# A graph layer on one Trainium2 core: node quarters chosen for each edge tile, seven sum slots a block for nine, and attention keys made in two steps a group

## The chip, the cores and the metric

One NeuronCore of a Trainium2 chip runs the program. Its engines work side by side and meet only through semaphores: TensorE (PE; its weight loads are shown as PEld), VectorE (DVE), ScalarE (ACT), GpSimd (POOL) and SyncE (SP). DMA transfers are issued from SP, ACT and POOL. The metric is the device time of one execution, in microseconds; the number given for a kernel is the median of its runs.

## The reference

Four layers follow one another over a table of 6,250 nodes of 256 values. Only the first one, and what prepares the second, is touched here:

```python
def _L0_gnn_ref(x, edge_index, edge_attr, u, batch, W1, b1, W2, b2):
    row, col = (edge_index[0], edge_index[1])
    h = jnp.concatenate([x[row], edge_attr], axis=1)
    h = jax.nn.relu(h @ W1 + b1)
    agg = jax.ops.segment_sum(h, col, num_segments=N_NODES)
    cnt = jax.ops.segment_sum(jnp.ones((h.shape[0],), h.dtype), col, num_segments=N_NODES)
    agg = agg / jnp.maximum(cnt, 1.0)[:, None]
    out = jnp.concatenate([x, agg], axis=1)
    return jax.nn.relu(out @ W2 + b2)
...
x = x + _L0_gnn_ref(_layernorm(x, axis=-1), edge_index, edge_attr_256, L0_gnn_u, batch0, L0_gnn_W1, L0_gnn_b1, L0_gnn_W2, L0_gnn_b2)
```

There are 106,250 edges, sorted by their destination `col`. For each edge the row of its source node is fetched, multiplied by one half of `W1`, added to the edge's attributes times the other half, passed through relu, and summed into the destination node. The second layer is a graph attention over 131,072 other edges with experts behind it; the third is a graph layer again over the first edges; the fourth is a mixture of experts. All is computed in float32.

## The kernel before

**Blocks, tiles, groups.** The nodes are cut into T = 49 blocks of P = 128. Since the edges are sorted, the edges of a block lie in one window: 18 tiles (CW) of 128 edges, beginning where the block's edges begin. A tile's edges are compared with the block's 128 node numbers (`equal`, L1211), which gives a matrix `eq` of 0 and 1, edges by nodes. The sum over edges is then a matmul: `eq` as the stationary operand, the edges' rows `h` (256 values and a 1 for the count) as the moving one, added up in one PSUM tile `pe` (`add_up`, L1522).

**Quarters.** Sorted edges also mean that the first tiles of a window hit only the first nodes of the block. So the 18 tiles are divided into six sets of three (NR, NT), and `QUARTERS` (L904) says which quarters of the block (32 nodes each) a set can hit. For each tile and quarter there is one matmul of 32 stationary columns, 33 in a block. The last block takes all 128 columns in one matmul of a tile. `load_windows` (L1183) counts how many edges lie inside their set's quarters; if the total isn't every edge, a slow general program runs behind this one.

**Groups.** Six tiles make a group (G1): set g and set g + 3. A block has NG = 3 groups, the layer 147. One turn of the main loop (L1632) has one number q and touches several groups at once: it joins group q-1, multiplies the attributes of group q, sums group q-2, starts the gathers of group q+2, turns the attributes of group q+1, and compares the edges of group q.

- `load_sources` (L1491): six indirect DMAs from POOL, each of 128 rows of 1 KB from `y_dram` into one of four buffers `h0` to `h3` (`ring`). A buffer is free when `add_up` of the group four before has read it.
- `load_attr` (L1401): the edge attributes, eight DMAs from SP and ACT into `ea`, three buffers.
- `turn` (L1497): DVE transposes `ea` into `et`. `hidden` (L1505): PE multiplies it with `w1b` into `ph` (two buffers of PSUM), in three parts of a turn (L1636, L1647, L1651).
- `join` (L1515): DVE adds `ph` to the gathered rows, ACT applies relu, in place.
- `add_up` (L1522): PE sums. In the old order of the loops, tile by tile from behind, the matmuls of the two sets alternate.
- `end_of` (L1547): after a block's third group, the mean, the second matmul and the first steps of the attention, spread over the following turns with `yield`.

**Work on the side.** `work`, `sort` and `slow` are lists of generators; `steps` (L1622) asks each for one step. `slow` finds and loads the windows of the next seven blocks. `sort` (L1614) prepares the attention: `make_keys` (L1259) packs source and destination of each attention edge into one number, in 8 x 6 = 48 steps, each a few DVE instructions on 128x128; `sort_steps` (L1295) sorts each partition's 1,024 numbers, in 100 steps of one or two DVE instructions; and `sorted_edges` (L1318) takes the result apart: nine DVE instructions on 128 x 640 to 848, five PE transposes, each with a copy by ACT into `lt` and a DMA to `low_dram`, and 160 short memsets with four comparisons. One step a turn: 148 steps and the tail for 149 turns.

**Order.** `Ordered.pin` (L35) ties each engine's instructions to the order in which the program was written, turn by turn. So an instruction that waits holds up all that stand behind it on its engine. In a turn PE has: part 0 of `hidden`, the sort's transposes if there are any, the sums, part 2, steps of `end_of`, part 4. DVE has: the join, a sort step, the turn of the attributes, steps of `end_of`, the comparisons, a window step. After the loop the layer's pools are given back and the attention starts, with the experts' matmuls of the second layer (L1715, L1731) between.

Of the kernel before, what the change touches and what calls it, by code (L numbers as in the profile page):

```python
# [8 lines left out]
F32 = mybir.dt.float32  # L9
# [7 lines left out]
P = 128  # L17
# [851 lines left out]
def kernel(ctx: ExitStack, tc: tile.TileContext, a: dict, out: bass.AP):  # L869
# [24 lines left out]
    CW = 18  # L894
# [7 lines left out]
    NR = CW // NT  # L902
    Q = P // 4
    QUARTERS = ((0, 1), (0, 2), (1, 3), (1, 4), (2, 4), (3, 4))  # L904
    H, X = a["L0_ffn_att_src"].shape
    HX = H * X
    GW = HX + 2 * H
# [36 lines left out]
    with ExitStack() as fast:  # L944
# [182 lines left out]
        def gather(dst, table, idx):  # L1127
            GP.indirect_dma_start(  # L1128
                out=dst, out_offset=None, in_=table[0:NP, :],
                in_offset=IndirectOffsetOnAxis(ap=idx, axis=0),  # L1130
            )

        def load_windows(b, pool):

            sl = slice(b * TB, (b + 1) * TB)
            n = TB * CW

            def flat3(v):
                return v.rearrange("p w a t -> p w (a t)")

            raw = {k: wix.tile([P, P], I32, name=f"raw_{k}") for k in ("src", "dst")}
            for w in range(b * TB, (b + 1) * TB):
                at, r = (w - b * TB) * CW, start_of(w)
# [38 lines left out]

            n = TB - (b == NB - 1)  # L1183
            for k, (lo, hi) in enumerate(QUARTERS):
                for limit, op in ((lo * Q - 0.5, OP.is_gt), (hi * Q - 0.5, OP.is_lt)):
                    if 0 < limit < P - 1:
                        V.scalar_tensor_tensor(
                            inside[:, :n, k, :], d[:, :n, k, :], limit, inside[:, :n, k, :],
                            op0=op, op1=OP.mult,
                        )  # L1190
# [20 lines left out]
        def equal(pool, w, q):  # L1211


            total = NT * Q * sum(hi - lo for lo, hi in (quarters(w, q), quarters(w, q + NG)))
            if w < T - 1:
                eq = pool.tile([P, EQ], F32, name="eq", bufs=3)
            else:
                eq = pool.tile([P, total], F32, name="eq4", bufs=1)
            found, at = {}, 0
            for k in (q, q + NG):  # L1220
                lo, hi = quarters(w, k)
                n = (hi - lo) * Q
                found[k] = eq[:, at : at + NT * n].rearrange("p (t n) -> p t n", n=n)
                at += NT * n
                V.tensor_tensor(
                    found[k], lane[:, None, lo * Q : hi * Q].to_broadcast([P, NT, n]),
                    dst1[:, w, k, :].unsqueeze(2).to_broadcast([P, NT, n]), op=OP.is_equal,
                )
            return found
# [88 lines left out]
        def sorted_edges(pst, wk):  # L1318
# [12 lines left out]
            for c in range(KA // P):  # L1331
                pt = pst.tile([P, 4, P], F32, name="pt")
                TE.transpose(pt[:, 0, :], some[:, c * P : (c + 1) * P], ident)
                lt = wk.tile([P, P], BF16, name="lt")
                SC.activation(lt, pt[:, 0, :], AF.Copy)
                SC.dma_start(low_dram[c * P : (c + 1) * P, :], lt)
            V.tensor_reduce(good2[:, 1:2], good3[:, :, 0], axis=AX.X, op=OP.add)
# [17 lines left out]
        with ExitStack() as layer:  # L1355
# [40 lines left out]
                return both  # L1396

            V.memset(gtab[:, :, HX : HX + H], 1.0)
            groups1 = [(w, g) for w in range(T) for g in range(NG)]

            def load_attr(q):  # L1401

# [66 lines left out]
            with (  # L1469
# [12 lines left out]
                last_of = [  # L1482
                    max(k % NG for k, (lo, hi) in enumerate(QUARTERS) if lo <= b < hi)
                    for b in range(4)
                ]
                NQ1 = len(groups1)

                def rows_of(q):
                    return ring[q % len(ring)]

                def load_sources(q):  # L1491

                    w, g = groups1[q]
                    for j, (k, t) in enumerate(chunk(g)):
                        gather(rows_of(q)[:, j, 0:D], y_dram, src1[:, w, k, t : t + 1])

                def turn(q):  # L1497

# [22 lines left out]

                def add_up(q):  # L1522

                    w, g = groups1[q]
                    if g == 0:
                        sums[w] = pse.tile([P, WS], F32, name="pe")
                    h, eq = rows_of(q), equals.pop(q)

                    for j in reversed(range(NT)):
                        for i, k in ((1, g + NG), (0, g)):  # L1530
                            lo, hi = quarters(w, k)
                            if hi - lo == 4:
                                TE.matmul(
                                    sums[w], eq[k][:, j, :], h[:, i * NT + j, 0:WS],
                                    start=g == 0 and j == NT - 1 and i == 1,
                                    stop=g == NG - 1 and j == 0 and i == 0,
                                )
                                continue
                            for b in range(lo, hi):
                                at = slice((b - lo) * Q, (b - lo + 1) * Q)  # L1540
                                TE.matmul(  # L1541
                                    sums[w][b * Q : (b + 1) * Q, :], eq[k][:, j, at],
                                    h[:, i * NT + j, 0:WS], start=g == 0 and j == NT - 1,
                                    stop=g == last_of[b] and j == 0,
                                )

                def end_of(w):  # L1547

# [64 lines left out]

                def sorting():  # L1614

                    yield from make_keys(wk)
                    yield from sort_steps()
                    sorted_edges(psm, wk)

                work, sort, slow = [], [sorting()], [windows()]  # L1620

                def steps(*more):  # L1622
                    for some in (*more, work):
# [2 lines left out]
                                some.remove(n)  # L1626

                for q in range(3):
                    load_sources(q)
                turn(0)  # L1630
                ordered = Ordered(tc)
                for q in range(NQ1 + 2):  # L1632
                    if 0 < q <= NQ1:
                        join(q - 1)
                    if q < NQ1:
                        hidden(q, 0)  # L1636
                    steps(sort)
                    if q >= 2:
                        add_up(q - 2)
                        if (q - 2) % NG == NG - 1:  # L1640
                            work.append(end_of((q - 2) // NG))
                    if 3 <= q + 2 < NQ1:
                        load_sources(q + 2)
                    if q + 1 < NQ1:
                        turn(q + 1)
                    if q < NQ1:
                        hidden(q, 2)  # L1647
                    steps()
                    if q < NQ1:
                        equals[q] = equal(wk, *groups1[q])  # L1650
                        hidden(q, 4)  # L1651
# [1019 lines left out]
```

## Time and profile before

| What | us |
|---|---|
| median of 3 runs (lowest, highest) | 3426.5 (3418.49, 3428.24) |
| the profiled execution, its own time | 3420.78 |
| its span, first to last instruction | 3418.8 |
| PE busy over the span | 3161.6 (92%) |
| DVE busy | 2156.1 (63%) |
| ACT busy | 1121.4 (33%) |
| POOL busy | 2245.7 (66%) |

The first layer's stream runs from about 104 us, when the first attributes are multiplied, to about 1277 us, when the last sum is done. The busy digits over 40 slices show it as the first 15 slices: PE at 8 and 9 tenths, DMA at 9, about 200 GB/s. In the last 1,000 us of the program the granted clock of PE is lower (5 to 7 tenths in the slices), which belongs to later layers.

How the rows are to be read: a row of the costliest groups has the line, the engine, the operation, the tile written and the tiles read, the shape and how often; then the busy time, the mean duration of one in ns, and the idle time of that engine just before such instructions with what ended most of it. "issue" means that nothing which the profile shows was waited for. A matmul of float32 has two records; records overlap, so the step from one to the next, not the duration of one, is what a matmul costs. Most matmuls stand under the line of a helper (L1115, L1109), gathers under L1128, and are told apart by their tiles.

### The profile page before, as it was taken

The numbers are of one execution on the slowest core, as the hardware profiler recorded it, in microseconds if no ns is written. First come the engines' busy times: TensorE is split into PE (matmuls) and PEld (weight loads), VectorE is DVE, ScalarE is ACT, GpSimd is POOL, SyncE is SP. The second block draws the span as 40 slices with busy tenths as digits, with TensorE's granted clock in tenths as the row PEclk, the third lists the DMA queues.
The fourth block names the chain that finished last, engine by engine and source line by source line (L and its number), as shares of the span: only waits on it lengthen the run. The fifth ranks groups of instructions, "written<-read, shape, count | busy, mean of one in ns | idle before, by whom it ended". The sixth has DMA issues, their size and how long they took to land.

```text
span 3418.8 us, 57189 instructions
## 1 busy us (share of the span) xinstructions
PE 3161.6 (92%) x18509; PEld 2529.4 (74%) x18509; DVE 2156.1 (63%) x5685; ACT 1121.4 (33%) x2010; POOL 2245.7 (66%) x2364
## 2 busy tenths in 40 slices
PE   7899999999999989999999999995678888988998
PEld 5677777777777767888888888883556665666776
DVE  5677787777666767877575758775334444545464
ACT  4122222222222224445545455661012112111134
POOL 0677777777777736766565556625777777777773
PEclk8999999999999999999999999996577777778698
DMA  6999999999999953334343434443112222222221
GB/s 190 199 210 204 199 199 206 200 199 203 206 208 207 207 119 102 98 87 132 85 118 99 132 85 132 113 100 88 53 54 59 60 59 60 59 59 65 60 63 39
DMA packets 698912, 428.56 MB, mean 125 GB/s; under 512 B 531272, under 2 KB 640315, under 8 KB 698604
## 3 DMA queue, kind: packets, MB, share of 16 engines
q0 software_dynamic: 89408, 178.08, 22.9%
q1 hardware_dynamic: 365948, 187.21, 21.0%
q10 hardware_dynamic: 243248, 59.52, 9.6%
q8 instruction: 150, 2.46, 0.3%
q14 instruction: 158, 1.29, 0.1%
HBM read 382.05 MB, written 42.49 MB: 124 GB/s over the span
## 4 chain that ended last, share of the span: by engine, by line
PE 65%; POOL 13%; DMA 9%; issue 6%; DVE 4%; ACT 2%; SPq 0%; ACTq 0%; POOLq 0%; DVEq 0%
PE ph L1115 33%; POOL hg L1128 12%; PE py L1115 11%; DMA hg<-hp_dram,src 6%; PE pe L1541 6%; PE po L1884 5%; PE pt L1115 4%; PE pe L2526 2%; DMA rb<-low_dram 2%; PE pa L1821 1%; PE pm L1115 1%; PE pt L1109 1%; POOL h L1128 1%; DMA h<-y_dram,src 1%; DVE x_all L2065 1%
## 5 line engine op out<-in xcount | busy, mean ns | idle before, releaser
L1128 POOL DMA_INDIRECT h<-y_dram,src x882 | 844.0, 957 | 395.0 <-issue 263.8
L1128 POOL DMA_INDIRECT hg<-hp_dram,src x831 | 784.5, 944 | 268.9 <-issue 221.2
L1128 POOL DMA_INDIRECT sg<-gat_dram,src x640 | 612.3, 957 | 353.0 <-issue 161.3
L1115 PE MATMUL ph<-w1b,et 128*128 128x256 f32 x3528 | 825.6, 386 | 10.4 <-DVE et L1500 9.9
L1115 PEld LDWEIGHTS ph<-w1b,et 128*128 128x128 f32 x3528 | 657.5, 191 | 153.6 <-issue 70.2
L2526 PEld LDWEIGHTS pe<-eq,hg 128*128 128x128 f32 x2036 | 392.8, 256 | 306.1 <-issue 134.4
L2526 PE MATMUL pe<-eq,hg 128*128 128x96 f32 (+15 forms) x2036 | 451.1, 351 | 159.0 <-DMA hg<-hp_dram,src 135.9
L1519 ACT ACTIVATE h<-h 128x1536 f32<-128x1536 f32 x147 | 218.2, 1485 | 586.5 <-DMA h<-y_dram,src 203.8
L2503 DVE TENSOR_SCALAR eq<-px,dst,ew 128x96 f32<-128x96 f32 x831 | 262.0, 367 | 232.5 <-PE pe L2526 142.4
L1518 DVE TENSOR_TENSOR h<-ph,h 128x1536 f32<-128x1536 f32 x147 | 258.3, 1757 | 228.2 <-PE ph L1115 208.4
L1115 PE MATMUL py<-w,hh 128*128 128x256 f32 x1568 | 385.6, 386 | 5.4 <-ACT hh L1720 4.9
L1115 PE MATMUL ph<-b_all,w 128*128 128x256 f32 (+1 forms) x1600 | 386.9, 381 | 2.9 <-issue 2.8
L1115 PEld LDWEIGHTS py<-w,hh 128*128 128x128 f32 x1568 | 290.6, 192 | 41.9 <-ACT hh L1720 6.9
L1115 PEld LDWEIGHTS ph<-b_all,w 128*128 128x128 f32 x1600 | 291.3, 191 | 36.2 <-issue 3.2
L1500 DVE STREAM_TRANSPOSE et<-ea 128x1536 f32<-128x1536 f32 x147 | 260.9, 1775 | 14.8 <-DMA ea<-in_edge_attr_dram 8.9
L1720 ACT ACTIVATE hh<-ph,b 128x256 f32<-128x256 f32 (+1 forms) x400 | 166.0, 466 | 289.0 <-PE ph L1115 276.2
L1884 PE MATMUL po<-pp,B 128*128 128x240 f32 (+10 forms) x1280 | 252.1, 337 | 1.9 <-DVE acc L1890 1.8
L1884 PEld LDWEIGHTS po<-pp,B 128*128 128x128 f32 x1280 | 215.5, 190 | 14.1 <-DVE acc L1890 2.6
L1541 PE MATMUL pe<-h,eq 128*32 128x257 f32 x3168 | 216.8, 384 | 0.0
L1863 DVE TENSOR_TENSOR pp<-px,A 128x960 f32<-128x960 f32 (+10 forms) x160 | 155.8, 974 | 3.9 <-PE po L1884 3.5
L1541 PEld LDWEIGHTS pe<-h,eq 128*32 128x32 f32 x3168 | 95.9, 109 | 83.9 <-issue 30.5
L1720 ACT ACT_TABLE_LOAD x98 | 125.7, 1283 | 49.7 <-PE ph L1115 47.1
(339 smaller groups left out, 3762.6 us busy)
## 6 DMA issues: line engine op xcount, KB each, us to landing
ea<-in_edge_attr_dram SPq DMA_DIRECT2D x588, 96.0 KB
ea<-in_edge_attr_dram ACTq DMA_DIRECT2D x588, 96.0 KB
y<-y SPq DMA_DIRECT2D x196, 128.0 KB
w<-in_L_ffn_W_dram SPq DMA_DIRECT2D x48, 512.0 KB
y<-ys SPq DMA_DIRECT2D x96, 256.0 KB
rb<-low_dram SPq DMA_DIRECT2D x80, 256.0 KB
h<-y_dram,src POOLq DMA_INDIRECT x882
hg<-hp_dram,src POOLq DMA_INDIRECT x831
```

Of the source, the lines that this page charges most:

```text
L1109: TE.transpose(pt[:, c, :], src[:, c * P : (c + 1) * P], ident)
L1115: TE.matmul(dst, lhs(c), rhs(c), start=c == 0, stop=c == n - 1)
L1128: GP.indirect_dma_start(out=dst, out_offset=None, in_=table[0:NP, :], in_offset=IndirectOffsetOnAxis(ap=idx, axis=0),)
L1500: V.transpose(et[q].rearrange("p c m k -> p m c k"), ahead.pop(q).rearrange("p i m (c k) -> p (i m) c k", c=2),)
L1518: V.tensor_add(h, ph.pop(q), h)
L1519: SC.activation(h, h, AF.Relu)
L1541: TE.matmul(sums[w][b * Q : (b + 1) * Q, :], eq[k][:, j, at], h[:, i * NT + j, 0:WS], start=g == 0 and j == NT - 1, stop=g == last_of[b] a ...
L1720: SC.activation(hidden[u][:, f, :n, :], ph[:, f - f0, :n, :], AF.Gelu, bias=b1[:, e, f : f + 1],)
L1863: V.tensor_tensor(pps[g, half][:, :, 0:n, :], pay[:, js, :].unsqueeze(2).to_broadcast([P, HG, n, HV]), near[g][:, js, 0:n].unsqueeze(3).to ...
L1884: TE.matmul(po.rearrange("p b v -> p (b v)"), B[:, j, :], pp[:, j, 0:n, :].rearrange("p b v -> p (b v)"), start=half == 0 and j == 0, stop ...
L2503: V.tensor_scalar(equals[k][:, j, :], lanes[:, 0:NW], dst_of[:, t : t + 1], ew[:, t : t + 1], op0=OP.is_equal, op1=OP.mult,)
L2526: TE.matmul(sums[b][:, lo - t0 * P : hi - t0 * P], hg[:, j, :], eq[:, j, lo - n0 : hi - n0], start=False, stop=after >= (t0 + n) * P,)
```

## The change

1. Each tile gets its own set of quarters (`reach`, from `RANGES`), 26 pairs of tile and quarter instead of 33. The test in `load_windows` goes over runs of tiles with the same limit.
2. The groups of a block are taken in the order 2, 0, 1 (`TURNS`). A plan made once (`planned`) hands out the pairs: 2, 2 and 3 slots (`SLOTS`) in the three turns, a slot having at most one matmul for each quarter. What doesn't fit, at most the third tile of either set (`LATE1`), is summed one or two turns later; so its rows and its part of `eq` are kept on.
3. `load_sources` is called twice a turn: for the tiles in `LATE1` of group q+1, then for the other four of group q+2.
4. `eq` has four buffers instead of three, the last block uses two of them in place of `eq4`, and `lt` has one buffer instead of two.
5. `make_keys` is a list of its own, `keys`, of which a turn takes two steps, one before the sums and one after part 2 of `hidden`. The sort starts when it is done.

```diff
-    groups1 = [(w, g) for w in range(T) for g in range(NG)]
+    TURNS, SLOTS = (2, 0, 1), (2, 2, 3)
+    RANGES = (((0, 1), 3), ((0, 2), 2), ((1, 2), 2), ((1, 3), 3), ((2, 3), 1), ((2, 4), 3), ((3, 4), 4))
+    reach = [r for r, n in RANGES for _ in range(n)]
+    groups1 = [(w, g) for w in range(T) for g in TURNS]
...
-            for k, (lo, hi) in enumerate(QUARTERS):
-                for limit, op in ((lo * Q - 0.5, OP.is_gt), (hi * Q - 0.5, OP.is_lt)):
-                    if 0 < limit < P - 1:
-                        V.scalar_tensor_tensor(
-                            inside[:, :n, k, :], d[:, :n, k, :], limit, inside[:, :n, k, :],
+            for limit in range(1, 4):
+                for op, some in (
+                    (OP.is_gt, [j for j in range(CW) if reach[j][0] == limit]),
+                    (OP.is_lt, [j for j in range(CW) if reach[j][1] == limit]),
+                ):
+                    part = slice(some[0], some[-1] + 1)
...
-                eq = pool.tile([P, EQ], F32, name="eq", bufs=3)
-            else:
-                eq = pool.tile([P, total], F32, name="eq4", bufs=1)
+                if eq is None or w == T - 1:
+                    eq, at = pool.tile([P, EQ], F32, name="eq", bufs=4), 0
...
-                lt = wk.tile([P, P], BF16, name="lt")
+                lt = wk.tile([P, P], BF16, name="lt", bufs=1)
...
+                def planned():
+                    left, plan, first, final = [[] for _ in range(4)], [], {}, {}
+                    for i, g in enumerate(TURNS):
+                        for j, (k, t) in enumerate(chunk(g)):
+                            for b in range(*reach[k * NT + t]):
+                                left[b].append((i, j, k, t))
+                        for n in range(SLOTS[i]):
+                            for b in range(4):
+                                if left[b]:
+                                    plan.append((i, b, *left[b].pop(0)))
...
+                LATE1 = (NT - 1, 2 * NT - 1)
+                EARLY1 = tuple(j for j in range(G1) if j not in LATE1)
...
-                    for j in reversed(range(NT)):
-                        for i, k in ((1, g + NG), (0, g)):
-                            lo, hi = quarters(w, k)
...
-                            for b in range(lo, hi):
-                                at = slice((b - lo) * Q, (b - lo + 1) * Q)
-                                TE.matmul(
-                                    sums[w][b * Q : (b + 1) * Q, :], eq[k][:, j, at],
-                                    h[:, i * NT + j, 0:WS], start=g == 0 and j == NT - 1,
+                    for i, b, own, j, k, t, start, stop in plan:
+                        if i == turn:
+                            of = q - turn + own
+                            lo = QUARTERS[k][0]
+                            TE.matmul(
+                                sums[w][b * Q : (b + 1) * Q, :],
+                                equals[of][k][:, t, (b - lo) * Q : (b - lo + 1) * Q],
+                                rows_of(of)[:, j, 0:WS], start=start, stop=stop,
...
                 def sorting():
-                    yield from make_keys(wk)
                     yield from sort_steps()
                     sorted_edges(psm, wk)
-                work, sort, slow = [], [sorting()], [windows()]
+                work, keys, sort, slow = [], [make_keys(wk)], [sorting()], [windows()]
...
-                    steps(sort)
+                    steps(keys or sort)
                     if q >= 2:
                         add_up(q - 2)
...
+                    if 3 <= q + 1 < NQ1:
+                        load_sources(q + 1, LATE1)
                     if 3 <= q + 2 < NQ1:
-                        load_sources(q + 2)
+                        load_sources(q + 2, EARLY1)
...
-                    steps()
+                    steps(keys)
```

More of the change, by code (lines that the diff above doesn't have):

```diff
@@ L1183, in load_windows @@
             n = TB - (b == NB - 1)
-            for k, (lo, hi) in enumerate(QUARTERS):
-                for limit, op in ((lo * Q - 0.5, OP.is_gt), (hi * Q - 0.5, OP.is_lt)):
-                    if 0 < limit < P - 1:
-                        V.scalar_tensor_tensor(
-                            inside[:, :n, k, :], d[:, :n, k, :], limit, inside[:, :n, k, :],
-                            op0=op, op1=OP.mult,
-                        )
+            tiled, at = (v.rearrange("p w a t -> p w (a t)") for v in (inside, d)), 0
+            tiled = list(tiled)
+            for limit in range(1, 4):
[4 more added lines that the diff above has]
+                    part = slice(some[0], some[-1] + 1)
+                    assert len(some) == some[-1] + 1 - some[0]
+                    V.scalar_tensor_tensor(
+                        tiled[0][:, :n, part], tiled[1][:, :n, part], limit * Q - 0.5,
+                        tiled[0][:, :n, part], op0=op, op1=OP.mult,
+                    )
             if n < TB:
@@ L1211, in equal @@
         def equal(pool, w, q):
-            total = NT * Q * sum(hi - lo for lo, hi in (quarters(w, q), quarters(w, q + NG)))
-            if w < T - 1:
-                eq = pool.tile([P, EQ], F32, name="eq", bufs=3)
-            else:
-                eq = pool.tile([P, total], F32, name="eq4", bufs=1)
-            found, at = {}, 0
+            eq, found, at = None, {}, 0
             for k in (q, q + NG):
@@ L1480 @@
                 equals, et, ph, sums = {}, {}, {}, {}
[L1482 to L1485, printed above, removed]
+                def planned():
[8 more added lines that the diff above has]
+                                    plan.append((i, b, *left[b].pop(0)))
+                        assert all(v[0] == i and v[1] in LATE1 for some in left for v in some)
+                    assert not any(left)
+                    for n, v in enumerate(plan):
+                        first.setdefault(v[1], n)
+                        final[v[1]] = n
+                    return [
+                        (*v, n == first[v[1]], n == final[v[1]]) for n, v in enumerate(plan)
+                    ]
+                LATE1 = (NT - 1, 2 * NT - 1)
+                EARLY1 = tuple(j for j in range(G1) if j not in LATE1)
+                plan = planned()
                 NQ1 = len(groups1)
@@ L1489, in rows_of, with load_sources @@
                     return ring[q % len(ring)]
-                def load_sources(q):
+                def load_sources(q, some):
                     w, g = groups1[q]
                     for j, (k, t) in enumerate(chunk(g)):
-                        gather(rows_of(q)[:, j, 0:D], y_dram, src1[:, w, k, t : t + 1])
+                        if j in some:
+                            gather(rows_of(q)[:, j, 0:D], y_dram, src1[:, w, k, t : t + 1])
                 def turn(q):
@@ L1522, in add_up @@
                 def add_up(q):
[L1524 to L1525 removed]
+                    w, turn = groups1[q][0], q % NG
+                    if turn == 0:
                         sums[w] = pse.tile([P, WS], F32, name="pe")
[L1527 to L1545 removed]
+                    if w == T - 1:
+                        for j, (k, t) in enumerate(chunk(TURNS[turn])):
+                            TE.matmul(
+                                sums[w], equals[q][k][:, t, :], rows_of(q)[:, j, 0:WS],
+                                start=turn == 0 and j == 0, stop=turn == NG - 1 and j == G1 - 1,
+                            )
+                        return
+                    for i, b, own, j, k, t, start, stop in plan:
+                        if i == turn:
+                            of = q - turn + own
+                            lo = QUARTERS[k][0]
+                            TE.matmul(
+                                sums[w][b * Q : (b + 1) * Q, :],
+                                equals[of][k][:, t, (b - lo) * Q : (b - lo + 1) * Q],
+                                rows_of(of)[:, j, 0:WS], start=start, stop=stop,
+                            )
                 def end_of(w):
@@ L1628 @@
                 for q in range(3):
-                    load_sources(q)
+                    load_sources(q, range(G1))
                 turn(0)
```

## The prediction, made before the changed kernel had run

> **What bounds the kernel now.** The change touches only the first layer, so I read that stage by itself: first the table of busy time by stretches, then the chain of waits inside it, then the instructions in order of time. In the table each engine has its busy us and, in brackets, its instructions; the last three columns are granted clock, DMA share and GB/s.
>
> ```profile
> 104.00:250.00 146.00, 138.81 (x912) 106.23 (x911) 112.36 (x221) 37.99 (x56) 110.65 (x117) 0.99 1.05 205
> 800.00:1240.00 440.00, 440.00 (x2945) 342.69 (x2939) 308.19 (x515) 126.09 (x211) 328.85 (x344) 1.00 0.96 203
> 1240.00:1300.00 60.00, 47.51 (x249) 38.54 (x247) 30.91 (x228) 19.14 (x43) 1.30 (x3) 0.91 0.24 67
> ```
>
> From 800 to 1240 us PE is never idle. POOL, the fifth engine, looks free with 328.85 of 440 us, but it isn't:
>
> ```profile
> L1128 POOL DMA_INDIRECT h<-y_dram,src x882 | 844.0, 957 | 395.0 <-issue 263.8
> L1541 PE MATMUL pe<-h,eq 128*32 128x257 f32 x3168 | 216.8, 384 | 0.0
> ```
>
> A gather takes 957 ns and 263.8 us / 882 = 0.30 us of issue before it: 1.256 us, so 18 gathers a block take 22.6 us. The order of time shows the gathers one behind the other, with one short wait:
>
> ```profile
> 1206.55 0.94 POOL L1128 DMA_INDIRECT h<-y_dram,src  x1 [0.30 <-issue]
> 1207.80 0.95 POOL L1128 DMA_INDIRECT h<-y_dram,src  x1 [0.30 <-issue]
> 1209.32 0.94 POOL L1128 DMA_INDIRECT h<-y_dram,src  x1 [0.58 <-issue]
> ```
>
> The third starts 1.52 us after the second, not 1.25: the sums of a block (until 1208.55 below) had to give it its buffer. PE's own period is in the chain:
>
> ```profile
> 1192.53 3.65 PE ph L1115 x16
> ...
> 1207.11 1.44 PE pe L1541 x24
> 1208.55 5.38 PE ph L1115 x24
> 1214.15 1.43 PE pe L1541 x18
> 1215.58 3.65 PE ph L1115 x16
> ```
>
> The same piece comes back after 1215.58 - 1192.53 = **23.05 us**, PE's block. POOL's 22.6 stands 0.45 us under it. So PE is the bound, and POOL is right behind. DMA is not third in line: in the packets an edge-attribute tile lands some 14 us before it is turned, although the share is 0.96.
>
> **Part 1: seven slots for nine.** Four 32-column matmuls, one for each quarter of the nodes, run side by side. The 24 records of a group (12 matmuls, two records each) take 1.44 us; 18 records (3 quarters) take 1.43. So a group costs three slots, however many quarters are in each. One record: (5.38 - 3.65) / 8 = 0.216 us from the ph rows, the same step as between the records of a slot in the trace; a slot is 2 x 0.216 = 0.432 us, and 1.44 - 3 x 0.432 = 0.14 us of entry stays. Before: 3 + 3 + 3 slots. After: 2 + 2 + 3, with 6 + 8 + 12 = 26 matmuls instead of 33. Removed: 2 x 0.432 x 48 blocks = **41.5 us of PE**; the last block is summed with whole matmuls as before. PE's block becomes 23.05 - 0.86 = 22.19 us, **under POOL's 22.6**. POOL makes the same 882 gathers, so POOL is late next.
>
> Neither the comparisons that make `eq` nor the window tests change in cost (six tests for seven, 176 ns each, seven times: 1 us of DVE, hidden below PE). The sets hold every edge of the inputs: I counted all 106,250 in them, so the general path is not entered.
>
> **Part 2: gathers in two parts, tiles kept for a group longer.** Tiles 2 and 5 of a group are now gathered one step later and stand in the order two of them, then four of the next. Same instructions, same queue. From the sum that frees the buffers to the join that needs the late tiles there are two steps instead of three, but they are first in the queue: 2 x 1.25 + 2.8 us of landing (mean over all gathers, from the packets; 5.3 us at the 99th percentile). PE needs the join's `ph` buffer 18.9 us after the release (two and a half steps of 7.4), and 6.4 us of DVE work stand before that in DVE's order (the join, sort steps, block end, turn), so they may land 12.5 us after it. With 5.3 that leaves about 7 us for POOL to be behind. I cost it at nothing; without that cover every landing tail costs its excess, about 2 us.
>
> The new cost is waits. In the program before, one gather of a group waits for PE; now five or six of six do: 668 waits on PE instead of 143. For POOL, the nearest row is the last layer's gathers (hg), of which every sixth waits for a DMA and PE: the trace has a semaphore instruction of 17 ns there, and the distance to the gather ahead stays 1.245 us, like the rest (1.249). So 0; upper end 0.1 us each, if POOL doesn't hide it (rival D). For PE, the Trainium skill speaks against this (TensorE: Matmul & The Clock Gate, "The cost: per-tile semaphore tail"): increments from matmuls serialize, 26.3 ns each. By it, 525 more increments cost 13.8 us of PE, 0.29 a block. The row: at the end of a ph group a matmul that increments is followed 0.215 us later, the usual step, so 0. I take the row; by the page PE's block would be 22.48, still under POOL's 22.6, so the sum would hardly differ.
>
> **Part 3: keys in two steps a group.** 48 key steps of 0.84 us DVE (152 instructions, 40.3 us in the trace) go into 24 groups instead of 48. DVE has 112.36 of 146 us there, 77%; 0.84 more in 7.6 us makes 88%: hidden behind PE and POOL, 0 to 2 us if DVE's order holds back a turn. But the sort behind them (100 steps) then ends at group 125 of 147 instead of in the last step, and with it the tail that sorts out the edges moves **from the end into the middle of the stream**. What it does at the end now:
>
> ```profile
> 1257.42 1.75 DVE L1518 TENSOR_TENSOR h<-ph,h 128x1536 f32<-128x1536 f32 x1
> ...
> 1262.57 0.49 DVE L1321 TENSOR_SCALAR src<-order 128x640 int32<-128x640 int32 x1
> ...
> 1267.42 0.60 DVE L1330 CAST low<-key 128x848 bf16<-128x848 f32 x1
> ```
> ```profile
> 1267.81 0.28 ACT L1335 ACTIVATE lt<-pt 128x128 bf16<-128x128 f32 x1 [4.44 <-PE pt L1333]
> ...
> 1269.68 0.28 ACT L1335 ACTIVATE lt<-pt 128x128 bf16<-128x128 f32 x1 [0.88 <-DMA low_dram<-lt]
> ...
> 1272.34 4.82 PE L1533 MATMUL pe<-h,eq 128*128 128x257 f32 x12
> ```
>
> The last join ends at 1259.2; the last sum could start 1.5 us later (ACT's relu) and starts at 1272.34: 11.6 us. Experts' matmuls fill part of it. PE idles 60 - 47.51 = 12.5 us in this stretch, of which the tail holds some 7, and its five transposes 1: **8 us go**, since PE is full again afterwards.
>
> In the middle it costs more. Queued behind it on PE: the sum of group 123, which frees POOL's buffers. Conversions 5.4 us on DVE, of which PE covers 2 with matmuls; then five transposes, each waiting for ACT's copy, which waits for the landing of the copy before, since `lt` now has one buffer: 1.5 us at the end, when DMA was quiet (1268.12 to 1269.6), and I take 2 to 3 beside full traffic. 4 + 5 x 0.6 + 4 x 2.5 = **17 us of PE**, ends 10 and 25. POOL goes on for its 7 us of lead, so 10 us reach the end of the stage.
>
> **The sum,** from join to join of the profiled execution (first 108.3, last 1257.4):
> - blocks 0 to 7: before 188.5 us; POOL 8 x 22.7 = 182: 6 gained.
> - blocks 8 to 27, where loading windows disturbs every seventh: before 477.9; PE 477.9 - 20 x 0.86 = 460.6, POOL 453, partly absorbing one another: 462, 16 gained.
> - the last 20.7 blocks: before 476.4 (23.05 each); POOL 20.7 x 22.65 = 469, and 10 of the tail: 3 lost.
> - the end: 8 gained.
>
> 6 + 16 - 3 + 8 = 27; 3420.8 - 27 = 3394. The profiled execution lies 5.7 under the median of the runs (3426.5); I add half of that: **3397 us**. The rest of the program is untouched.
>
> **Rivals.**
> - A, the forecast, 3384 to 3412: chance 0.55.
> - B, POOL doesn't bind: its 1.25 us contain waits that shrink, and its lead swallows the tail (5 us left): 41.5 + 8 - 5 = 45, so 3379. For it: the gathers' median step is 1.251, 22.5 a block. Against: 22.5 is still over 22.19. 0.17.
> - C, nothing to measure: the tail costs 25 us of PE, none absorbed, and keys and late tiles 4: 6 + 16 + 8 - (25 + 4 - 7) = 8 gained, 3416. For it: PE, ACT and DVE wait for one another there, with one buffer each. 0.16.
> - D, slower: POOL pays for the added waits. Some 12 gathers of a block at 0.1 us: 22.65 + 1.2 = 23.85, over 48.7 blocks 1161 us against 1149, and 10 - 8 for the tail: 14 lost, 3437. It decides from 0.076 us a wait. For it: where a gather really waits, 0.3 us go. Against: the hg row. 0.10.
> - E, 0.02: a set of quarters misses edges and the slow path runs; the count speaks against it.
>
> Under 0.3% (10 us) this kernel can't be told from no change. Faster: A, B and a little of C, 0.75; same 0.13; slower 0.12. The range 3375 to 3424 leaves out D and half of B.
>
> **What would show it.** The sums have 2,496 records in 128x32 form, in pieces of 12, 16 and 24. Right: gathers 1.25 to 1.27 us apart through the stage, PE idle some 0.4 us a block, blocks of 22.6; one hole of 10 to 25 us on PE around 1060 us; the last sum within 4 us of the last join. Wrong: blocks of 22.2 (B), gathers over 1.33 apart (D), blocks still 23.05 (the slots cost no less).

## The result and the profile after

The changed kernel takes **3401.09 us** (median of 5 runs, 3400.27 to 3405.05), the kernel before on the same chip 3422.54 (median of 5, 3418.49 to 3428.24; the 3426.5 given ahead is the median of three of them): ratio 0.9939, 95% interval 0.9924 to 0.9954, 21 us or 0.6% faster. The profiled execution's span fell from 3418.8 to 3401.3, by 17.5 us.

First the two groups of the costliest list that the change touches (busy us, mean ns of one, then the idle time just before them and what ended it).

```profile
L1131 POOL DMA_INDIRECT h<-y_dram,src x882 | 848.8, 962 | 393.6 <-issue 197.3 <-DMA ea<-in_edge_attr_dram 92.0 <-PE pe L1564 48.8
L1564 PE MATMUL pe<-h,eq 128*32 128x257 f32 x2496 | 178.4, 390 | 0.0
```

The sums fell from 3,168 records to 2,496. The gathers are as many and as long as before. 48.8 us of their idle time is now put down to waits for PE's sums. Part of this is no added cost, since 0.30 us stands before any gather; the rest are longer waits, like the one of 7.29 us shown further down. The same stretches as before the change:

```profile
104.00:250.00 146.00, 137.38 (x836) 105.37 (x836) 126.30 (x284) 38.43 (x57) 110.61 (x117) 0.98 1.01 207
800.00:1240.00 440.00, 423.52 (x2648) 329.70 (x2647) 305.67 (x647) 126.45 (x211) 326.20 (x338) 0.98 0.98 201
1240.00:1300.00 60.00, 56.91 (x338) 48.37 (x337) 31.91 (x92) 24.61 (x50) 20.50 (x22) 0.97 0.41 109
```

In the first, DVE's 112.36 has become 126.30 (the keys, twice as dense); in the second, PE, which was never idle, is idle for 16.5 us in all; in the third, PE has 56.91 instead of 47.51. The chain in an undisturbed stretch gives PE's block:

```profile
1134.79 3.65 PE ph L1118 x16
...
1141.89 1.00 PE pe L1564 x16
1142.90 5.38 PE ph L1118 x24
...
1148.49 1.44 PE pe L1564 x24
...
1156.97 3.65 PE ph L1118 x16
```

1156.97 - 1134.79 = **22.18 us** for 23.05. Two of the three pieces of sums now take 1.00 us instead of 1.43, the third 1.44. The gathers beside them, in order of time, come 1.25 us apart, also the one for which a wait for the sums is recorded (0.30 us, as where nothing is waited for):

```profile
1147.53 0.95 POOL L1131 DMA_INDIRECT h<-y_dram,src  x1 [0.30 <-issue]
...
1148.79 0.95 POOL L1131 DMA_INDIRECT h<-y_dram,src  x1 [0.31 <-PE pt L1112]
...
1150.04 0.95 POOL L1131 DMA_INDIRECT h<-y_dram,src  x1 [0.30 <-PE pe L1564]
```

So the slots cost what they were priced at, 0.86 us a block or 41.5 us in all, while the whole change gained 21. By the joins' starts in the trace (times between joins, so that each stretch can be compared; the last join began at 1257.42 and at 1251.84):

| Stretch | before | after | gained | predicted |
|---|---|---|---|---|
| up to the first join | 108.25 | 106.63 | 1.6 | 0 |
| blocks 0 to 7 | 188.48 | 188.93 | -0.5 | 6 |
| blocks 8 to 27 | 477.87 | 474.08 | 3.8 | 16 |
| block 28 to the last join | 482.8 | 482.2 | 0.6 | -3 |
| last join to the end | 2161.4 | 2149.4 | 12.0 | 8 |

The tail is where it was expected. In the instructions by time (in brackets the idle time before each, with what ended it):

```profile
1077.03 0.45 PE L1339 MATMUL pt<-ident,key 128*128 128x128 f32 x1 [5.77 <-DVE key L1335]
...
1080.40 0.28 ACT L1341 ACTIVATE lt<-pt 128x128 bf16<-128x128 f32 x1 [2.61 <-DMA low_dram<-lt]
...
1086.86 0.69 PE L1112 MATMUL pt<-ident,o 128*128 128x128 f32 x2 [1.36 <-ACT lt L1341]
...
1087.48 1.94 PE L1564 MATMUL pe<-h,eq 128*32 128x257 f32 x12
...
1089.28 1.40 POOL L1131 DMA_INDIRECT h<-y_dram,src  x1 [7.82 <-issue]
```

PE waits 5.8 us for the conversions, then for each transpose's copy, whose `lt` waits for the store ahead (2.61 us the longest). The sum behind them begins at 1087.48, and POOL, its lead used up, has stood for 7.8 us (the row puts this down to "issue"; that it waits for the sum is read from the order). This block takes 39.95 us, **17.8 more** than 22.18. At the end the reverse:

```profile
1251.84 1.76 DVE L1544 TENSOR_TENSOR h<-ph,h 128x1536 f32<-128x1536 f32 x1 [3.94 <-DMA h<-y_dram,src]
...
1256.93 2.77 PE L1555 MATMUL pe<-h,eq 128*128 128x257 f32 x12
...
1277.35 0.95 POOL L1131 DMA_INDIRECT sg<-gat_dram,src  x1 [4.27 <-DMA hp<-in_src_dram]
```

The last sum follows the last join's end by 3.3 us instead of 13, and the attention's first gather comes 25.5 us after the join's start instead of 41.8 (1299.20 in the trace of before).

### The profile page after: what moved, and what is told of

The parts are those of the page before. It is cut to its first block, busy times and chain, and to the rows that moved or that the text cites. A ratio compares the mean times of both kernels' runs of the same rounds, so it can differ in the third digit from the quotient of the medians.

```text
span 3401.3 us, 56400 instructions
## 1 busy us (share of the span) xinstructions
PE 3126.4 (92%) x17837; PEld 2510.2 (74%) x17837; DVE 2154.8 (63%) x5678; ACT 1121.5 (33%) x2010; POOL 2251.3 (66%) x2364
## 4 chain that ended last, share of the span: by engine, by line
PE 56%; DMA 15%; POOL 13%; issue 7%; DVE 5%; ACT 2%; SPq 1%; ACTq 0%; POOLq 0%; DVEq 0%
PE ph L1118 28%; POOL hg L1131 12%; PE py L1118 11%; DMA hg<-hp_dram,src 6%; PE po L1908 5%; DMA ea<-in_edge_attr_dram 4%; PE pe L1564 4%; PE pt L1118 3%; DMA h<-y_dram,src 3%; PE pe L2550 2%; DMA rb<-low_dram 2%; PE pa L1845 1%; DVE et L1526 1%; PE pt L1112 1%; PE pm L1118 1%
## 5 line engine op out<-in xcount | busy, mean ns | idle before, releaser
L1118 PEld LDWEIGHTS ph<-w1b,et 128*128 128x128 f32 x3528 | 658.6, 191 | 160.9 <-issue 75.0
L1564 PE MATMUL pe<-h,eq 128*32 128x257 f32 x2496 | 178.4, 390 | 0.0
L1118 PE MATMUL py<-ew,g 65*128 65x256 f32 x392 | 132.7, 469 | 1.0 <-DVE miss L2640 1.0
```

The lines of the kernel that those rows point to most:

```text
L1118: TE.matmul(dst, lhs(c), rhs(c), start=c == 0, stop=c == n - 1)
L1564: TE.matmul(sums[w][b * Q : (b + 1) * Q, :], equals[of][k][:, t, (b - lo) * Q : (b - lo + 1) * Q], rows_of(of)[:, j, 0:WS], start=start, s ...
```

## Where the gain of blocks 8 to 27 went

The table of stretches, cut at the joins of these 20 blocks, first of the kernel before, then of the changed one (busy PE, PEld, DVE, ACT, POOL; then clock, DMA share, GB/s):

```profile
296.73:774.60 477.87, 468.11 (x3093) 361.83 (x3094) 360.48 (x699) 131.12 (x221) 343.35 (x359) 0.99 0.99 201
```
```profile
295.56:769.65 474.09, 453.21 (x2813) 352.60 (x2814) 357.74 (x668) 130.62 (x221) 344.45 (x358) 0.98 1.04 202
```

PE does 14.9 us less and is idle 20.9 us instead of 9.8: most of what the slots gave came back as idle PE. Neither is it POOL at its limit: 344.45 us of gathers and 358 x 0.30 of issue are 451.9 of 474.1. The idle time stands in a few places, every 14 turns, where SP loads the windows of the next seven blocks with 14 small transfers (`raw_src`, `raw_dst`, L1149). There are four such batches in these blocks, and the waits of PE for ACT beside them, 3.53, 4.33, 1.77 and 6.80 us, are 16.4 of the 20.9 us; in the kernel before they are 2.04, 0.67 and 2.75 us at three of the batches, 5.5 together. The longest one of the changed kernel, in order of time:

```profile
728.05 5.28 ACTq L1416 DMA_DIRECT2D ea<-in_edge_attr_dram  x4
...
731.59 0.28 SPq L1149 DMA_DIRECT2D raw_dst<-in_dst_dram  x1
...
733.60 1.48 ACT L1545 ACTIVATE h<-h 128x1536 f32<-128x1536 f32 x1 [11.32 <-DMA raw_src<-in_src_dram]
...
735.41 2.08 PE L1118 MATMUL pt<-w,b_all 128*128 128x256 f32 x4 [6.80 <-ACT o L1113]
...
742.15 0.94 POOL L1131 DMA_INDIRECT h<-y_dram,src  x1 [7.29 <-PE pe L1564]
```

ACT's four issues of edge attributes take 5.28 us; two turns later, undisturbed, 1.89. Its relu, whose join was ready at 730.4, and its copy of `o` stand behind them, PE waits 6.80 us for the copy, POOL 7.29 us for the sum behind that. And PE then starts slowly:

```profile
735.40:741.20 5.80, 5.79 (x16) 4.51 (x16) 1.62 (x5) 1.60 (x2) 0.00 (x0) 0.62 1.25 207
741.20:760.00 18.80, 18.80 (x126) 14.56 (x125) 12.22 (x21) 5.00 (x10) 13.57 (x15) 1.00 0.82 184
```

The granted clock is 0.62 in the 5.8 us after the wait, 1.00 after that. The Trainium skill has a rule for this (TensorE: Matmul & The Clock Gate, "Why this matters for your kernels"): no idle gap of PE over some 3 us, or the clock falls back. The trace agrees for this gap, but the limit is not sharp here: in the changed kernel the clock was 1.00 in the 6.4 us after the wait of 3.53 us, and in the kernel before it was 0.68 in the 5.3 us after the one of 2.04:

```profile
405.38 1.40 PE L1115 MATMUL pt<-w,b_all 128*128 128x256 f32 x4 [2.04 <-ACT o L1110]
```
```profile
405.40:410.70 5.30, 5.30 (x16) 4.08 (x16) 2.20 (x8) 1.48 (x2) 1.92 (x3) 0.68 1.22 227
```

From here the theory to test, **T**: the slots' gain is given back by these loads (30.5 us over 20 x 22.18 in blocks 8 to 27, where the kernel before lost 16.9 over 20 x 23.05), by the tail's 17.8 us, and by POOL's limit of about 22.6 us a block once its lead is gone. Against it stand D (the added waits and late gathers cost time themselves), R (POOL sets the pace, so the tail's place doesn't matter) and W (the loads are not the cause).

## The experiments

**The loads spread** (loads_spread). A pair of loads a turn, instead of 14 in one turn:

```diff
                     SY.dma_start(v[at : at + CW, :], rows)
-            for _ in range(3):
-                yield
+                yield
+            yield
```

> The changed kernel with the 14 loads of a batch of windows (raw_src, raw_dst, issued by SP in one step, 1.5 us each) spread over seven steps, a pair each. Theory T: the long blocks (25 to 31 us, about every fifth up to block 27) come from SP standing in these loads, so that ACT's edge-attribute issues, and its relu and copies behind them, come late: they shrink to below 24 us each, blocks 8 to 27 take 450 to 460 us instead of 474: 3380 to 3390 us. Rival W (the long blocks come from the windows' arithmetic on DVE, or from the gathers that stand late in POOL's queue): 3397 to 3405 us.

Measured: 3383.53 us, ratio 0.9875 (0.9859 to 0.9892). Blocks 8 to 27:

```profile
287.41:743.48 456.07, 448.88 (x2817) 350.14 (x2816) 348.99 (x636) 131.16 (x220) 346.75 (x359) 1.00 1.03 209
```

18 us less than in the changed kernel, at a clock of 1.00, and now POOL is at its limit: 346.75 + 359 x 0.30 = 454.5 of 456.07. A little of this is only moved: the batches now come every 19 turns, three of them instead of four in these blocks, and blocks 28 to 40 take 297.7 us instead of 292.6. From the first join to the last it is 1122.9 us for 1145.2. T holds, W falls. ACT's four issues of edge attributes take at most 4.34 us in these blocks, where five groups of the changed kernel took 5.2 to 6.2, three of them beside the loads. What ties ACT's issues to SP's loads, the profile does not show.

**PE's work cut** (half_hidden). The matmuls of `hidden` take one chunk instead of two, so half of the product is left out and the values are no longer the layer's:

```diff
-                            lambda c: w1b[:, c, :],
+                            lambda c: w1b[:, c, :], 1,
```

> The changed kernel with half of the hidden product of the edge attributes left out (one of two chunks of 128 columns), which takes 36 x 0.216 = 7.8 us from PE's block: PE cannot bind. Theory T: POOL is the next bound right above PE, undisturbed blocks of 22.5 to 22.7 us with gathers 1.25 us apart and PE idle about 8 us in each. Rival: DVE or the transfers bind, blocks over 23 us; or POOL's step itself holds waits that PE caused, blocks below 22.2 us.

Measured: one run, 3385.56 us. With PE's block shortened by a third the time is no better than with the loads spread. Blocks 28 to 40 (after the loads, before the tail) take 22.55 us each. So POOL is the next bound, where the prediction had it; the changed kernel itself takes 22.51 in these blocks. Blocks 8 to 27:

```profile
293.30:751.72 458.42, 345.12 (x2097) 229.85 (x2098) 356.14 (x668) 130.53 (x221) 343.36 (x356) 0.88 1.09 208
```

The loads are bunched here, yet the 20 blocks take 458, not 474: a PE that is idle for 5.7 us in each block, (458.42 - 345.12) / 20, makes most of the delays good, a PE with 0.4 us to spare doesn't. The 8 us of idle time that were expected did not come; the clock is 0.88 here.

**Nine slots again** (nine_slots_b), all else as changed:

```diff
-    reach = [r for r, n in RANGES for _ in range(n)]
+    reach = [QUARTERS[j // NT] for j in range(CW)]
-    TURNS, SLOTS = (2, 0, 1), (2, 2, 3)
+    TURNS, SLOTS = (2, 0, 1), (3, 3, 3)
```

> The same kernel as nine_slots (nine slots again, late gathers, added waits and two key steps kept), once more. Theory T: undisturbed blocks of 23.05 us, the long block near 1090 us of 40 us, the end 12 us shorter: 3422 to 3431 us. Rival D (added waits and late gathers cost by themselves): blocks over 23.2 us, 3434 to 3442. If the slots were not what made the changed kernel faster: 3401.

Measured: 3420.6 us, ratio 0.9982 (0.9975 to 0.9989), just under T's range and clear of D's. Undisturbed blocks are 23.05 us to the hundredth, so the late gathers and the added waits cost nothing there; the block of the tail takes 39.38. The 20 blocks:

```profile
299.57:773.64 474.07, 466.09 (x3093) 360.60 (x3094) 358.34 (x667) 131.33 (x221) 344.00 (x358) 1.00 0.97 202
```

474.07 us, the changed kernel's 474.08, with 12.9 us more of PE work. By these two traces, one of each kernel, **the seven slots are worth nothing in blocks 8 to 27**; their gain is made outside: 10.3 us from block 28 to the last join (492.5 and 482.2; 20.7 x 0.86 would be 18, POOL keeps the rest) and 3.1 in blocks 0 to 7. By the ratios the two kernels differ by 0.43%, 15 us. Why the same delays of ACT (four issues in 5 us at each batch in this kernel too) leave PE 8.0 us of idle time with nine slots and 20.9 with seven, no run shows. I can only argue: with a shorter block PE comes sooner to what waits for ACT.

**The keys undone** (keys_one_b), slots and gathers as changed:

```diff
                 def sorting():
+                    yield from make_keys(wk)
                     yield from sort_steps()
...
-                work, keys, sort, slow = [], [make_keys(wk)], [sorting()], [windows()]
+                work, keys, sort, slow = [], [], [sorting()], [windows()]
```

> The same kernel as keys_one (the changed kernel, one key step a group again), once more, because the first four ran on a chip on which the kernel before took 4234 us. From the runs since then POOL is known to set blocks of about 22.55 us where its lead is gone. Theory T: no long block near 1060 us, the end from the last join 12 us longer, POOL takes back 3: 3398 us, 3394 to 3403. Rival R: 3408 to 3413.

Measured: 3413.41 us, ratio 0.9959 (0.9944 to 0.9974): R's number, not T's. The intervals of this and of the changed kernel overlap; by the medians the keys in two steps are worth some 7 us, which is not clear of the noise. The trace says how. The long block is gone (22.26 us), and the stretch from block 28 to the last join is 10.7 us shorter than in the changed kernel, not 15: without the hole, in which POOL regains its lead, blocks 41 to 47 take 22.96 us each, where the changed kernel's six after the hole take 22.18. And the end is longer by 17.3 us, not 12:

```profile
1255.77 0.48 PE L1339 MATMUL pt<-ident,key 128*128 128x128 f32 x1 [4.50 <-DVE key L1335]
...
1264.54 4.10 PE L1555 MATMUL pe<-h,eq 128*128 128x257 f32 x12
...
1289.11 0.95 POOL L1131 DMA_INDIRECT sg<-gat_dram,src  x1 [5.97 <-ACT rest L1940]
```

The last join began at 1245.74, the first gather of the attention comes 43.4 us later (25.5 in the changed kernel). So the tail is cheaper in mid-stream than at the end; T's balance of the two places was wrong, its account of the hole was not. But this kernel has `lt` in one buffer at the end too: its five copies by ACT begin within 7.4 us, from 1256.3 to 1263.7, where two buffers took 3.7 in the kernel before. Against that kernel the end gained 12.0 us, little more than the 10.7 of the hole.

**The tail spread too** (both_spread). Beside the spread loads `sorted_edges` becomes a generator, with a `yield` after `src2`, each conversion and each transpose, and around the limits:

```diff
                 SC.dma_start(low_dram[c * P : (c + 1) * P, :], lt)
+                yield
...
-                    sorted_edges(psm, wk)
+                    yield from sorted_edges(psm, wk)
```

> The changed kernel with both the tail of the sort and the loads of the windows spread over steps. Theory T: both gains, some of it taken back by POOL, whose 18 gathers a block take 22.6 us: from first to last join 48.7 x 22.6 = 1100 us is the least, against 1145; 3368 us, 3362 to 3378. If POOL or the lead of the late gathers set the pace (rivals R and D): 3385 us or more.

Measured: 3378.47 us, ratio 0.9863 (0.9847 to 0.988), 5 us less than with the loads alone, with intervals that overlap; T had 15. The one long block became three: blocks 41 to 43 take 25.04, 29.47 and 28.73 us, together 83.2 for 84.7. The transposes show why:

```profile
1079.44 0.26 ACT L1343 ACTIVATE lt<-pt 128x128 bf16<-128x128 f32 x1
...
1079.75 0.69 PE L1112 MATMUL pt<-ident,o 128*128 128x128 f32 x2 [2.64 <-ACT lt L1343]
```

The one PSUM buffer `pt` serves the tail and the block end. Each transpose holds it until ACT, busy with a relu, has copied it, and the block end's own transposes wait for that in PE's order.

**The transposes put where `pt` is free** (tail_aligned), one in every third turn:

```diff
+        step = [0]
...
             for c in range(KA // P):
+                while step[0] % NG:
+                    yield
                 pt = pst.tile([P, 4, P], F32, name="pt")
...
                 for q in range(NQ1 + 2):
+                    step[0] = q
```

> The kernel both_spread with the five transposes of the tail put only into the step of each block in which the block end has just left the one buffer pt and takes it again 6 us later (every third step). Theory P (spreading the tail gained only 5 us because each transpose held pt, whose copy stands behind ACT's relu of the join, while the block end's own transposes waited for it): blocks 41 to 43, which took 25.04, 29.47 and 28.73, fall to below 24 each, POOL's 22.55 stay: 3364 to 3372 us. Rival R (POOL sets the pace, the tail's place doesn't matter): 3375 to 3382 us, like both_spread.

Measured: **3372.73 us**, ratio 0.985 (0.9831 to 0.9869), just above P's range, and the lowest median of all kernels here: 1.5% under the kernel before, where the change as made is 0.6% under it. Its interval overlaps that of the kernel before this one, so the times alone don't settle P against R; the blocks do. Blocks 41 to 43 take 25.06, 22.57 and 22.14 us, the first over P's 24. Its transposes lie in blocks 42 to 46, so the whole tail is to be read from blocks 41 to 47: 173.4 us with the tail in one piece (loads_spread), 172.6 in eleven, 160.9 now; seven undisturbed ones would be 7 x 22.18 = 155.3. From block 28 to the last join:

```profile
745.26:1219.85 474.59, 463.93 (x2907) 363.10 (x2906) 341.92 (x732) 136.82 (x233) 356.38 (x369) 1.00 1.01 208
```

474.59 us for 485.3 in the kernel before this one, and POOL busy with 356.38 + 369 x 0.30 = 467.1 of it. Most of what is left belongs to POOL.

**On other chips.** Six of the runs fell on two chips on which every kernel, the one before too, takes some 24% longer (4234.56 and 4240.09 us in the two sets), with instructions of about the usual length in the traces from there (a gather 952 to 965 ns for 957, a record of `ph` 394 to 405 for 386), DMA packets that are no longer (those of the gathers' queue 128 to 132 ns in the mean, for 140), and idle time for which the profile names "issue" or an unknown queue. Sizes in us can't be carried over from there. Two of the kernels are those of the diffs above (keys_one, nine_slots); tail_spread is the changed kernel with the tail's `yield`s alone, loads_before the kernel before with the loads' alone, and keys_only, run twice, the kernel before with this:

```diff
-                lt = wk.tile([P, P], BF16, name="lt")
+                lt = wk.tile([P, P], BF16, name="lt", bufs=1)
...
                 def sorting():
-                    yield from make_keys(wk)
...
-                work, sort, slow = [], [sorting()], [windows()]
+                work, keys, sort, slow = [], [make_keys(wk)], [sorting()], [windows()]
...
-                    steps(sort)
+                    steps(keys or sort)
...
                         hidden(q, 2)
-                    steps()
+                    steps(keys)
```

> The changed kernel with its third part undone: one key step a group again, so the sort and the tail behind it end where they did before. Theory T (undisturbed blocks take 22.18 us because PE lost 0.86 us each; of what this brings, 17.8 us are given back by the tail in mid-stream and the rest by the loading of windows; about 12 us come from the end): the long block near 1060 us (39.95 us in the changed kernel) goes, the end from the last join gets 12 us longer as before, and the last blocks, without the hole in which POOL caught up, lose about 3 us to POOL: 3401 - 17.8 + 3 + 12 = 3398 us, 3394 to 3403. Rival R (POOL sets the pace of the last 20 blocks and the hole costs only what POOL would have taken anyhow): the hole's going gains 0 to 5, the end loses 12: 3408 to 3413 us.

> The kernel before with only the third part: the keys in two steps a group, lt in one buffer, nine slots and gathers as they were. Theory T: blocks of 23.05 us, a hole of 15 to 18 us on PE near 1090 us, the end from the last join 12 us shorter: 3422.5 + 17 - 12 = 3427 us, 3422 to 3431. Rival R (POOL has 7 us of lead and swallows part of the hole): 3415 to 3421 us. If the tail cost what it costs at the end, about 8 us, no more: 3418.

> The changed kernel with its first part undone: every tile again in all quarters of its run, 33 matmuls in 3+3+3 slots, but gathers in two parts, a wait on PE for most of them, four eq tiles and the keys in two steps. Theory T: blocks of 23.05 us, the same hole and the same end as with the keys alone: within 4 us of that kernel, about 3427 us. Rival D (the added waits and late gathers cost POOL or PE time): blocks over 23.2 us, 7 to 15 us slower than the keys alone, 3434 to 3442 us.

> The changed kernel with the tail of the sort (conversions, five transposes with copy and store, limits) cut into steps, one a group, instead of all in one group. Theory T: the block of 39.95 us becomes one or two of 23 to 25, 17.8 us less, of which POOL takes back about 3 and the small waits 2: 3388 us, 3384 to 3393. Rival R (POOL sets the pace there): no more than 5 us gained, 3396 to 3401 us.

> The kernel before with only the loads of the windows spread over steps. Known so far: with the loads bunched, blocks 8 to 27 take 474.07 us both with seven slots (the changed kernel) and with nine (nine_slots_b). Theory T (each batch of loads costs PE a hole; with nine slots the holes are about 17 us in 20 blocks): blocks 8 to 27 fall from 477.9 to 461 - 465, the rest stays: 3410 us, 3405 to 3415, and the seven slots are then worth 20 us or more beside it (the changed kernel with the same loads: 3383.5). Rival W (spread loads help only where PE has little to do): 3418 to 3426 us.

> The same kernel as keys_only (the kernel before with the keys in two steps a group alone), once more on whatever chip comes. Theory: within 3 us of nine_slots_b (3420.6 us, ratio 0.9982), since late gathers and added waits cost nothing: ratio 0.9975 to 0.9995, undisturbed blocks of 23.05, one long block of 39 to 41 us, the end 12 to 14 us shorter. Rival D (late gathers and waits cost some us, which the keys hide in nine_slots_b): ratio below 0.996.

Measured, as ratios to the kernel before on the same chip: the keys undone 1.0315 (1.0275 to 1.0355), the changed kernel with the tail spread 1.0309 (1.0283 to 1.0336), the keys alone 1.0047 (1.0029 to 1.0065) and 1.0025 (1.0 to 1.0049), nine slots with the rest 0.993 (0.9906 to 0.9953), the kernel before with the loads spread 1.0021 (1.0001 to 1.0041). So the keys alone, and the spread loads beside nine slots, could not be judged on the first kind of chip. For the second run of the keys alone a ratio of 0.9975 to 0.9995 by the theory, or below 0.996 by D, had been named for any chip, and neither came. The ratio of the spread loads lies on the side of its rival W, not of T, but where every block has other waits too this decides little, and what they bring beside nine slots stays open. One thing stands out: both kernels with seven slots lose 3% there, and the one with nine and all else as changed gains. What POOL waits for between 250 and 1050 us, first with nine slots, then with seven (the tail spread):

```profile
POOL h L1131 <- issue: 192.0, 426, 4.7
POOL h L1131 <- ACT b_all L1113: 41.2, 21, 2.3
POOL h L1131 <- ACT o L1113: 37.5, 17, 2.3
...
POOL h L1131 <- PE pe L1564: 1.5, 3, 0.9
```
```profile
POOL h L1131 <- issue: 201.3, 370, 8.2
POOL h L1131 <- PE pe L1569: 125.1, 35, 8.0
```

With nine slots a group's tiles are all summed in its own turn, so the buffers of the late tiles are free a turn before they are gathered into; with seven they come free only in the turn that fills them again. So POOL waits for PE, 125.1 us in 800, in 35 waits of up to 8.0 us. That this makes the 3%, I only argue: with nine slots 78.7 us are put down to ACT's copies, a row names only the last of several releasers, and no run there takes the late sums away alone. It is not D's price for each wait, since the kernel with nine slots has the late gathers and the added waits as well and gains. The changed kernel itself was not run there.

## Why the prediction was right

The forecast, 3397 us with a range of 3375 to 3424, was right in sign, and 4 us under the result. Most of its prices were right, one large term was not, and that the sum came so near is partly luck.

- **Part 1, the slot's price.** Right: 22.18 us a block for 22.19, and POOL is the next bound (22.55 us measured with PE relieved, 22.6 predicted). But blocks of 22.6 through the stage did not come: where POOL has lead, in blocks 29 to 33 and 42 to 47, they take 22.18, which the prediction named as a sign of B. POOL's limit takes its part only once the lead is gone.
- **Part 2, gathers and waits at 0.** Right on this chip: gathers 1.25 us apart, undisturbed blocks of 23.05 with nine slots. By the estimate from the Trainium skill's 26.3 ns for each of 525 increments, 0.29 us a block, these would have been 23.3: the row was the better guide. (Two and a half steps of 7.4 us are 18.5, not 18.9; nothing hung on it.) The cover that was named, the slack of the late tiles, may be what fails on the other chips.
- **Part 3, the tail in mid-stream.** Right: 17.8 us on PE for 17. "10 us reach the end of the stage" agrees with 10.7 by the keys undone. "8 us go" at the end was too small: 12.0 us against the kernel before, 17.3 against the keys undone. The term counted PE's idle time alone, and not that the attention's first gathers wait for the tail too.
- **Blocks 8 to 27, 16 gained.** This is the step that failed: 3.8. "Partly absorbing one another" took the disturbances as a sum that stays or shrinks when PE gets faster. They grew, from 16.9 to 30.5 us over PE's own time: the waits for ACT at the four batches from 5.5 to 16.4 us, and behind the two longest of these waits the clock fell, as it did behind two shorter ones before. With the loads spread these blocks take 456 us, where 462 was forecast. Why a shorter block makes the waits longer stays argued. The term for blocks 0 to 7 (6 gained, none measured) has the same fault.
- **The last 20.7 blocks, 3 lost.** 0.6 gained, but of "before 476.4" the last block was left out, which sums with whole matmuls: 482.8. POOL bound only in blocks 34 to 40 (22.83 us each). Before them it had lead left from the delays; after them the tail's hole gave lead back.

The errors of blocks 0 to 27 (18.7 us too much) stood against 4.0 at the end, 3.6 in the last blocks and 1.6 before the first join, and half the distance of the profiled execution to the median had been added; so the total is nearer than its terms. That these errors stood against one another was luck.

## What to carry to other kernels

A bound that is made shorter stops hiding the delays beside it: before counting a per-block gain over all blocks, look at the blocks that are already longer than the bound, and ask what delays them; here 20 of 49 blocks gave next to nothing until 14 small loads were spread over turns. Work moved off the end of a stage and into a stream held in order should go in as single steps, each at the place where its buffer is free: the same tail cost 18.1 us over blocks 41 to 47 in one piece, 17.3 in eleven pieces at the wrong places, and 5.6 at better ones.

## What the runs showed of the hardware

After a wait of 6.8 us PE's granted clock was 0.62 for the next 5.8 us, and eight records of `ph` then took 2.33 us instead of 1.97; in the 7 us after the tail it was 0.68. A wait of 3.53 us left it at 1.00, and one of 2.04 us in the kernel before was followed by 0.68. With half of the hidden product left to do, and gaps of up to 9.3 us between its pieces, PE's clock was 0.88 over 20 blocks. Two of the chips take 24% longer for the same program (4234.56 and 4240.09 us for 3422.54), with instructions and DMA packets of about the usual length; why, stays open.
